# Four stacked blocks on an image batch: the last gated output step and the first convolution half, put under the order of the program

## The chip, the cores and the metric

The kernel runs on one core of a Trainium2 chip. A core has five engines that run their own instruction streams side by side and wait for one another by semaphores: TensorE (PE, matrix products), VectorE (DVE), ScalarE (ACT), GpSimd (POOL) and SyncE (SP, which here only issues DMA transfers). The metric is the time of one execution on the device in microseconds (us), as a median of several runs.

## The reference, cut to what matters

The input `x` is a batch of 8 images of 56 x 56 positions with 192 channels, in float32. Four blocks follow one another, each of the form `x = x + block(group_norm(x))`:

```python
x = x + L0(_gn(x))   # gated Toeplitz mixing, 192 -> 576 -> 192 channels
x = x + L1(_gn(x))   # the same form with other weights
x = x + L2(_gn(x))   # 7x7 depthwise convolution, LayerNorm, 192 -> 768 (gelu) -> 192
x = x + L3(_gn(x))   # shifted window attention, 7x7 windows, 6 heads

def L1(x):           # what the change touches is its last line
    p, q, v = silu(x @ p_w.T + p_b), silu(x @ q_w.T + q_b), silu(x @ v_w.T + v_b)
    o = toeplitz_along_rows(q * v) + toeplitz_along_columns(q * v)
    return (p * o) @ o_w.T + o_b

def L2(x):           # and the first line of this one
    y = depthwise_conv_7x7(x)
    y = gelu(layernorm(y) @ w0 + b0) @ w1 + b1
    return y * gamma
```

## The kernel before, in words

Images go through in pairs: pair `j` is image `j` beside image `j + 4`, so that 192 channels of two images fill three rows of 128 partitions. Two pairs make a half: `j0 = 0` is the first half, `j0 = 2` the second. Each step of work is a Python generator that issues instructions for a while and then yields the time that its author gives to them; `weave` runs one lane of such steps and draws pieces of other work into it after each yield, by those times.

**The order.** All instructions are known when the kernel is built. A planner then sets the order of each engine's stream: it may issue an instruction ahead of others that the program wrote earlier, when its inputs are ready sooner by the planner's own estimates. Inside `tc.manual_schedule(engines=ENGINES)` the four engines PE, ACT, DVE and POOL keep the order in which the program wrote the instructions. SP is not in that set, and its order is the planner's throughout. Before the change such blocks surround the preparation of the tables, the four lanes with the Toeplitz step (`in_order` in `tno_layers`), and the last part of the attention. The fifth lane stands outside of them: `lanes[4]`, the output step `tno_out` of block L1 for the second half (`j0 = 2`), into which `last()` hands the convolution of block L2 for the first half.

**The output step** (`tno_out`) has 28 tiles of 224 positions. For each tile it issues `inner`: 16 matrix products with the gate's weights as 32 instructions (lines 536 and 545) into two PSUM buffers, four silu on ACT (L555), two products by the mixed signal on DVE (L560). Then comes `outer`: the rest of this tile's gate (L575, L581), the normalisation of the next tile's input on DVE (three instructions of L523), the output product of the tile before (L578, L586, L589, L592), one silu (L594) and its product (L595), then bias and residual (L598, L601), the store by POOL's queue (L122) and the statistics for the next group norm (L604). `inner` yields 4.9 and `outer` 5.8, and the convolution is drawn in at these yields. PSUM is cut into four buffers, handed out in turn (`bank2`).

**The convolution** (`conv`) has two kinds of step. A token step (`tokens`, 14 in a half: 7 of part 0 with 128 channels, 7 of part 1 with the other 64) takes a loaded tile `x`, normalises it on ACT (L805: four instructions in part 0, two in part 1), turns it by TensorE transposes (L817: 16 or 8) into PSUM and copies it to `xt` (L828 on DVE, and in part 0 L826 on ACT). There are two buffers of `x`; SP loads the next tile (L791 for part 0, L787 for part 1) when the transposes of the tile two steps back are done. A group step (`group`, 48 in a half) is 16 products by a banded matrix `cm` as 32 instructions (L837) and one ACT copy to `y` (L844). Eight groups fill `y`, of which there is one; POOL copies its border (L878) and stores it to `yd` (L879).

In the text of `tokens` the normalisation stands straight ahead of the transposes that read it:

```python
            for i in range(2 * n):
                j, k = (i, 2) if part else (i // 2, i % 2)
                nc.scalar.activation(x[:, i, :], x[:, i, :], AF.Identity, ...)
            for i in range(0, 4, 2):
                pt = self.bank2()
                ... nc.tensor.transpose(pt[...], x[:, k, ...], self.ident) ...
```

**Where the pieces fall.** Worked out from the yields and from `lo=0.08, hi=0.8` in `last()`, the token steps of part 0 stand after `inner` of tiles 2, 4 and 6 and after `outer` of tiles 2, 3, 4 and 5; those of part 1 after `inner` of tiles 11, 12 and 13, after `outer` of tiles 12 and 13, and two together after `outer` of tile 11. Groups 0 to 15 lie between the two parts, groups 16 to 47 after them, up to `inner` of tile 22. From there on the lane opens the MLP of block L2 (`mlp`, handed in as `after`): the load of `y` (line 920) after `outer` of tile 22, the first half of the LayerNorm statistics (L931, L932: 8 pairs of instructions on DVE) after `inner` of tile 23, the second half and the root (L935 on ACT, L936 on DVE) after its `outer`, and the normalisation (L943, 24 instructions on DVE) after `inner` of tile 24. `last()` also issues the loads of the MLP's vectors and four memsets of `xt` on POOL (L772, L773). After the lane follow the MLP with the second half of the convolution, in the planner's order.

Of the kernel before, what the change touches and what calls it, by code (L numbers as in the profile page):

```python
# [19 lines left out]
ENGINES = {  # L20
    mybir.EngineType.PE,
    mybir.EngineType.Activation,
    mybir.EngineType.DVE,
    mybir.EngineType.Pool,
}
# [13 lines left out]
def view(ap, offset, dims):  # L39

    return bass.AP(ap.tensor, ap.offset + offset, [ap.ap[0], *dims])


class Net:
# [636 lines left out]
    def tno_layers(self, x0, x1, x2, gn, last):  # L681


        tc, nc = self.tc, self.nc
        LS = ("L0", "L1")
        tables = [

            [
                self.dram.tile([D1 // 32 * self.TG + 1, 32 * self.TW], F32, name=f"{L}_tab{d}")
                for d in range(2)  # L690
            ]
            for L in LS
        ]
        qvs = {

            j0: self.dram.tile([D1 // 32, 64 * W, 128], F32, name=f"qv{j0}") for j0 in (0, 2)
        }
        o = [self.dram.tile([B // 2, 9, 128, T], F32, name=f"{L}_sum") for L in LS]
        x = (x0, x1, x2)
        with ExitStack() as ctx, ExitStack() as wqp:  # L700
            self.wqp = wqp.enter_context(tc.tile_pool(name="wqp", bufs=1, side="right"))
            self.tp = ctx.enter_context(tc.tile_pool(name="tp", bufs=3))
            Q = lambda i, j0, *more: self.tno_qv(LS[i], j0, x[i], gn[i], qvs[j0], *more)
            O = lambda i, j0, woven=True: self.tno_out(LS[i], j0, x[i], gn[i], o[i], x[i + 1], gn[i + 1], woven)
            TZ = lambda i, j0: self.tno_toeplitz(j0, tables[i], qvs[j0], o[i])
            QT, OT, TZT = 25 * 2.25 * 5.3, 28 * 10.7, 8 + 72 * 3.2

            with tc.tile_pool(name="tab", bufs=2) as tab:
                stats = [self.input_stats(x0, gn[0], j, tab) for j in range(4)]
                for more in stats[0]:  # L710
                    pass
                first, rest = Q(0, 0, tab, (0, 512)), Q(0, 0, None, (512, 2 * D1), 2)
                next(first)

                for n in range(14):
                    next(first)
                    next(stats[1], None)
                for more in stats[1]:
                    pass
                for n in range(10):  # L720
                    next(first)
                none = tab.tile([112, 512], F32, name="none", bufs=1)
                nc.gpsimd.memset(none, 0.0)
                for t in tables:
                    for d in range(2):
                        nc.gpsimd.dma_start(t[d][D1 // 32 * self.TG :, :512], none[:1])
                decay = [self.decay_tables(LS[i], tab, tables[i]) for i in range(2)]
                more = (dt for st in stats[2:] for dt in st)
                with tc.manual_schedule(engines=ENGINES):
                    for n in range(28):  # L730
                        next(more, None)
                        if n == 18:
                            next(rest)
                        if next(first, None) is None:
                            next(rest)
                        if n < 21:
                            next(decay[0])
                        if n >= 7:
                            next(decay[1])
                        if n in (14, 21):  # L740
                            qv = qvs[0 if n == 14 else 2]
                            to = qv[:, T:].rearrange("n (p k) e -> p n (k e)", p=112)
                            nc.gpsimd.dma_start(to, view(none, 0, [[0, D1 // 32], [1, 512]]))
                    for more in decay:
                        assert next(more, None) is None
                lanes = [[(rest, QT * 5 / 9 * 21 / 25 - 25.0), (Q(0, 2), QT)], [(O(0, 0), OT), (Q(1, 0), QT)]]
                parts = [Q(1, 2, None, cols) for cols in ((0, 512), (512, 2 * D1))]
                lanes += [[(O(0, 2), OT), (parts[0], QT * 4 / 9)], [(parts[1], QT * 5 / 9), (O(1, 0), OT)]]
                lanes += [[(O(1, 2, False), OT)]]
            in_order = tc.manual_schedule(engines=ENGINES)  # L750
            with tc.tile_pool(name="tz", bufs=1) as self.tz, in_order:
                self.tms = []
                for i in range(2):
                    self.tms.append(self.tz.tile([128, 32 * self.TW], F32, name=f"tm{i}"))
                for n, tz in enumerate((TZ(0, 0), TZ(0, 2), TZ(1, 0), TZ(1, 2))):
                    self.weave(lanes[n], tz, lanes[n + 1][0][0], TZT)
                wqp.close()
            self.weave(lanes[4], **last())

# [918 lines left out]
```

## Time and profile before

| what | value |
|---|---|
| median of 3 runs | 5438.96 us (5432.41 to 5443.45) |
| the profiled execution's own time | 5425.63 us |
| its span, first to last instruction | 5423.8 us |
| TensorE busy | 5166.0 us (95%) |
| VectorE, ScalarE, GpSimd busy | 48%, 44%, 33% |
| mean granted TensorE clock | 0.978 |
| fifth lane, from its first to its last matrix product | 3023.97 to 3540.4 us |

The page of a profile gives the busy time of each engine, then the span in 40 equal slices with one digit for each (9 is 90% or more busy), then the chain of work that ended last, then groups of instructions by source line. In a group, "out<-in" names the tiles, and behind the second bar stands how long the engine sat idle just before these instructions and what released it. Views of a stretch of time list the instructions in order: start, duration (of all `xN` together where several stand in one row), engine, line, operation, and in brackets the idle time before. PEld is the load of a weight into TensorE, which overlaps with products. Start and duration are in us from the span's start. Rows of one duration are pipelined, so the next instruction can start before the row's end.

### The profile page before, as it was taken

Reading aid. Unit: us, or ns where it says so; the run is one execution under the profiler, and the core shown is the slowest. Engines: PE = TensorE matmul, PEld = TensorE weight load, DVE = VectorE, ACT = ScalarE, POOL = GpSimd, SP = SyncE. Lnnn points to the kernel's source line nnn. Section 1 sums busy time; section 2 is a strip of 40 time slices with the busy share of each in tenths; the row PEclk is TensorE's granted clock in tenths of the full one; section 3 lists DMA queues with packets and bytes.
Section 4 is the critical chain, followed back from the end, with each engine's and each line's share of the span. In section 5 each row is a group of like instructions: output and inputs, shape, how many; then the busy total and the mean of one; then the engine's idle time right before and its main releaser. Section 6 shows DMA issues by size and latency. Waiting matters only on the chain.

```text
span 5423.8 us, 144350 instructions
## 1 busy us (share of the span) xinstructions
PE 5166.0 (95%) x64672; PEld 3811.2 (70%) x64672; DVE 2589.3 (48%) x3990; ACT 2383.5 (44%) x3179; POOL 1767.2 (33%) x1291
## 2 busy tenths in 40 slices
PE   7879999999999999999999899989999999999998
PEld 4657777777777777777777789856665444777776
DVE  6535556455555555555556422422222331566666
ACT  3345555444554454655455422243323333444443
POOL 2225675133664243546443100000000100333333
PEclk9889999999999999999999999999999999999998
DMA  7699997888786999889897667635454221445552
GB/s 251 151 243 283 289 311 234 265 281 267 241 262 176 307 317 318 279 226 291 285 312 266 205 223 248 229 96 190 135 174 124 75 68 49 85 98 108 101 102 68
DMA packets 1051146, 1116.48 MB, mean 206 GB/s; under 512 B 235200, under 2 KB 986304, under 8 KB 1036128
## 3 DMA queue, kind: packets, MB, share of 16 engines
q1 hardware_dynamic: 911584, 854.88, 52.9%
q0 software_dynamic: 38144, 200.99, 9.6%
q10 hardware_dynamic: 100800, 51.38, 3.9%
q8 instruction: 508, 8.32, 0.6%
q14 instruction: 110, 0.90, 0.1%
HBM read 743.17 MB, written 363.94 MB: 204 GB/s over the span
## 4 chain that ended last, share of the span: by engine, by line
PE 50%; DVE 3%; DMA 3%; issue 1%; ACT 1%; POOL 1%; SPq 0%; POOLq 0%; ACTq 0%; DVEq 0%
PE bank L980 7%; PE bank L837 5%; PE bank L1060 5%; PE bank L1254 4%; PE bank L263 4%; PE bank L592 3%; PE bank L1074 3%; PE bank L536 3%; PE bank L1370 2%; PE bank L1201 2%; PE bank L1284 2%; PE bank L1325 2%; PE bank L406 2%; PE bank L586 1%; PE bank L1344 1%
## 5 line engine op out<-in xcount | busy, mean ns | idle before, releaser
L263 PE MATMUL bank<-wq,t 128*128 128x256 f32 (+4 forms) x7680 | 1290.3, 374 | 72.1 <-DVE t L272 40.8
L263 PEld LDWEIGHTS bank<-wq,t 128*128 128x128 f32 (+2 forms) x7680 | 1005.2, 190 | 350.8 <-issue 92.4
L272 DVE TENSOR_TENSOR t<-bank,wq 128x1024 f32<-128x1024 f32 (+3 forms) x480 | 517.7, 1112 | 692.5 <-PE bank L263 537.1
L304 POOL TENSOR_TENSOR t<-t 128x1024 f32<-128x1024 f32 (+2 forms) x288 | 528.0, 1847 | 676.5 <-ACT t L301 339.1
L413 ACT COPY ot<-bank 128x896 f32<-128x896 f32 x576 | 493.4, 909 | 515.1 <-PE bank L406 401.8
L429 POOL TENSOR_TENSOR s<-s,ot 128x1568 f32<-128x1568 f32 x128 | 551.1, 4306 | 193.8 <-DVE ot L426 128.4
L301 ACT ACTIVATE t<-t 128x2048 f32<-128x2048 f32 (+2 forms) x288 | 423.0, 1488 | 328.8 <-DVE t L272 319.0
L406 PE MATMUL bank<-q,tm 56*32 56x224 f32 x18432 | 504.9, 353 | 22.0 <-DMA tm<-L_tab 10.6
L406 PEld LDWEIGHTS bank<-q,tm 56*32 56x32 f32 x18432 | 340.0, 106 | 148.2 <-issue 81.7
L122 POOL DMA_DIRECT2D x<-t x112 | 87.0, 777 | 1071.7 <-DVE t L601 1007.4
L560 DVE TENSOR_TENSOR t<-t,bank 128x896 f32<-128x896 f32 x224 | 242.8, 1088 | 401.6 <-ACT bank L555 346.0
L555 ACT ACTIVATE bank<-bank,wo 128x448 f32<-128x448 f32 x448 | 262.8, 605 | 377.4 <-PE bank L545 349.8
L980 PE MATMUL bank<-z,w 128*128 128x448 f32 (+1 forms) x1344 | 413.3, 555 | 2.8 <-DVE xt L828 2.8
L536 PE MATMUL bank<-t,wo 128*128 128x224 f32 x1792 | 375.9, 364 | 21.1 <-ACT t L515 10.6
L536 PEld LDWEIGHTS bank<-t,wo 128*128 128x128 f32 x1792 | 337.7, 194 | 51.7 <-issue 29.6
L592 PE MATMUL bank<-t,wo 128*128 128x224 f32 x1792 | 368.9, 359 | 0.0
L592 PEld LDWEIGHTS bank<-t,wo 128*128 128x128 f32 x1792 | 329.9, 190 | 31.1 <-issue 31.1
L980 PEld LDWEIGHTS bank<-z,w 128*128 128x128 f32 (+1 forms) x1344 | 183.0, 189 | 209.8 <-issue 199.5
L837 PEld LDWEIGHTS bank<-xt,cm 113*112 113x112 f32 x3072 | 309.7, 178 | 25.7 <-issue 23.3
L837 PE MATMUL bank<-xt,cm 113*112 113x108 f32 (+2 forms) x3072 | 316.0, 263 | 1.0 <-ACT h L989 1.0
L127 POOL DMA_DIRECT2D x<-x x64 | 36.7, 573 | 855.5 <-DVE x L1011 796.7
L424 DVE STREAM_TRANSPOSE s<-ot 128x1792 f32<-128x1792 f32 x144 | 292.8, 2034 | 24.5 <-ACT ot L413 16.2
(162 smaller groups left out, 6977.2 us busy)
## 6 DMA issues: line engine op xcount, KB each, us to landing
q<-qv SPq DMA_DIRECT2D x36, 3584.0 KB
t<-L_sum SPq DMA_DIRECT2D x112, 1008.0 KB
L_sum<-s POOLq DMA_DIRECT2D x256, 392.0 KB, 7.2
qv<-t SPq DMA_DIRECT2D x192, 512.0 KB
cm<-in_L_cm SPq DMA_DIRECT2D x96, 896.0 KB
tm<-L_tab SPq DMA_DIRECT2D x288, 240.0 KB
q<-qv SPq DMA_DIRECT2D x40, 1568.0 KB
q<-qv ACTq DMA_DIRECT2D x32, 1568.0 KB
```

The lines of the kernel that those rows point to most:

```text
L263: nc.tensor.matmul(pp[:m, b, 256 * j : 256 * j + k], x[rows, j, 2 if part else b, s : s + m], w[rows, part, c0 + c : c0 + c + k],  start=p ...
L272: nc.vector.tensor_add(z[:m, c : c + k, :], view(pp[:m], 0, [[1, k], [256, 4]]), view(bias[:m], c0 + c, [[1, k], [0, 4]]),)
L301: nc.scalar.activation(z[:m, :n, :], z[:m, :n, :], AF.Silu)
L304: nc.gpsimd.tensor_mul(prod[:m, :k], half[:, :, 0], half[:, :, 1])
L406: nc.tensor.matmul(pt[32 * j : 32 * j + 32, r, hf * 224 : (hf + 1) * 224], tm[rows, at : at + 32], q[rows, :, 4 * c : 4 * c + 4], start=Tr ...
L413: nc.scalar.copy(view(ot, 4 * (g % 4), [[16, 2], [32, 112], [1, 4]]), view(pt, 0, [[512, 2], [4, 112], [1, 4]]),)
L424: nc.vector.transpose(to, of.rearrange("p (i k) -> p i k", k=32))
L429: add.tensor_add(to, to, view(of, 0, [[1, 28], [32, 56]]))
L536: mm(gs[c // 2][:, b, c % 2 * 256 : c % 2 * 256 + N], pw[:, 0, 128 * c : 128 * c + 128], xn[:, b], start=c % 2 == 0, stop=False,)
L592: mm(P[:, b, :N], ow[:, c, 0:128], g[:, 4 * b + c], start=False, stop=c == 3)
L837: nc.tensor.matmul(pc[:, 128 * e + 4 * m0 : 128 * e + 4 * m1], cm[:113, e, k, :], xt[:, m0 - 1 + k : m1 - 1 + k, c + e, :], start=n == 0 a ...
L980: nc.tensor.matmul(phs[c][:, s, :TT], w0[rows, part, at : at + 128], z[rows, Z[2 if part else s], :], start=part == flip, stop=part != flip,)
```

## The change

The call of `weave` for the fifth lane is put into a block of its own in which PE, ACT, DVE and POOL keep the order of the program:

```diff
                 for n, tz in enumerate((TZ(0, 0), TZ(0, 2), TZ(1, 0), TZ(1, 2))):
                     self.weave(lanes[n], tz, lanes[n + 1][0][0], TZT)
                 wqp.close()
-            self.weave(lanes[4], **last())
+            with tc.manual_schedule(engines=ENGINES):
+                self.weave(lanes[4], **last())
```

`last()` is evaluated inside the block too, so its memsets belong to it. No instruction is added, removed or altered in its operands.

## The prediction

> **What bounds the kernel now.** I read the page first: the busy slices, and the chain that ended last.
>
> ```profile
> PE   7879999999999999999999899989999999999998
> ...
> PE 50%; DVE 3%; DMA 3%; issue 1%; ACT 1%; POOL 1%; SPq 0%; POOLq 0%; ACTq 0%; DVEq 0%
> ```
>
> TensorE is at nine tenths almost everywhere, and no other engine takes over 3% of the chain. So in the fifth lane (3023.97 to 3540.4) a wait of TensorE is paid in full, and nothing behind the lane has room to give it back: from 3551 to 4101 TensorE is busy 541.62 of 550 us. Then the windows of the lane:
>
> ```profile
> 3023.00:3122.00 99.00, 92.09 (x652) 77.29 (x653) 43.51 (x91) 48.89 (x81) 3.82 (x5) 0.95 0.53 176
> 3122.00:3225.00 103.00, 100.83 (x866) 92.56 (x866) 24.40 (x53) 20.05 (x37) 5.55 (x9) 1.00 0.67 240
> 3225.00:3272.00 47.00, 42.21 (x298) 34.83 (x296) 24.14 (x47) 14.93 (x25) 2.31 (x3) 0.96 0.59 206
> 3272.00:3473.00 201.00, 201.00 (x1746) 183.66 (x1743) 46.83 (x99) 47.22 (x83) 9.60 (x16) 1.00 0.72 252
> 3473.00:3541.00 68.00, 64.25 (x450) 52.17 (x448) 44.87 (x149) 19.94 (x32) 4.60 (x6) 1.00 0.49 153
> ```
>
> Columns are the stretch, its length, then PE, PEld, DVE, ACT, POOL, the granted clock and DMA. TensorE idles 6.9 and 4.8 us in the first and third stretch (the token steps of part 0 and part 1), 2.2 us in the second, nothing in the fourth (groups alone), 3.75 us in the last. The most that a better order can win is these 17.6 us and what a low clock costs after them.
>
> I compared TensorE's order of lines over the whole lane with the order in which the program writes the steps. They agree step for step: the transposes L817 and the products L837 stand where the yields put them. What the planner moved is on ACT and DVE. ACT in order of time:
>
> ```profile
> 3043.87 2.71 ACT L805 ACTIVATE x<-x,gn 128x448 f32<-128x448 f32 x4
> ...
> 3051.23 2.41 ACT L555 ACTIVATE bank<-bank,wo 128x448 f32<-128x448 f32 x4 [3.57 <-PE bank L545]
> ...
> 3081.54 0.76 ACT L805 ACTIVATE x<-x,gn 128x448 f32<-128x448 f32 x1 [3.92 <-DMA x<-x]
> ```
>
> By the program, L805 of the first token step comes behind the silu of 3051.23; here its last two instructions are among those of 3043.87, one to half a tile early. Over the lane L817 waits for L805 nowhere. The price of the early place is the third row: L805 stands ahead of a silu that is ready, and waits there for its transfer. TensorE pays:
>
> ```profile
> 3077.80 1.78 PE L545 MATMUL bank<-t,wo 64*128 64x224 f32 x16
> 3079.51 1.96 PE L817 MATMUL bank<-ident,x 128*112 128x128 f32 x16
> 3085.14 0.63 PE L575 MATMUL bank<-t,wo 64*64 64x224 f32 x1 [3.66 <-DVE t L560]
> ...
> 3092.82 1.91 PE L817 MATMUL bank<-ident,x 128*112 128x128 f32 x16
> 3094.57 0.73 PE L536 MATMUL bank<-t,wo 128*128 128x224 f32 x3
> ```
>
> **The change part by part.** No instruction is added; all cost is waiting.
>
> *Goes: the planner's own waits at the token steps.* Gaps of 3.66, 2.27, 0.76, 1.23, 0.76, 1.34 and 0.70 us, together 10.72, and slow products after two of them: `outer` from 3085.14 takes 7.68 us instead of 6.29, and the transposes and products from 3236.47 lose 0.18 + 1.78. That is 14.1 us off.
>
> *Comes: transposes behind their own normalisation.* In program order ACT runs L805 behind the silu of the half tile just done, and TensorE cannot pass its transposes.
> After `inner`: the silu end 1.77 us after its last product (3051.23 + 2.41 against 3051.87). Four L805 take 2.71, then the last of them lets 13 of 16 transposes go at 0.109 (1.75 over 16, the rows above): 1.42, with 0.1 for the semaphore. 6.0 us instead of 1.75: 4.25 lost, three times, 12.8.
> After `outer`: the silu L594 ends 0.62 after the last product (3073.13 + 0.42 against 3072.93), then the same 2.71 + 0.1 + 1.42: 4.85, so 3.1 lost, four times, 12.4.
> Part 1 has two L805 (1.40) and 8 transposes (0.87, of which 7 remain, 0.76). After `inner` 4.03 against 0.87: 3.16, three times, 9.5. After `outer` 2.88 against 0.87: 2.0, twice, 4.0; the pair behind tile 11 takes 0.62 + 2.80 + 0.1 + 0.76 = 4.28 against 1.74: 2.5.
> Sum 41.2 us. The low end is L805 alone, 7 x 2.71 + 7 x 1.40 = 28.8. The high end adds a transfer of `x` that is late twice, at 6.4 us each (the longest wait of L805 for it): 54. I take 41.2: the next load starts when the transposes two steps back are done, and landed some 6 us later (issued 3094.81, read 3100.60), while a step lasts at least half a tile, 4.85 or 6.29, plus its own wait.
>
> *The clock behind these waits.* Stretches without matrix products in this lane and what the following products lost: 3.57 us before 3023.97 cost 3.1 (6.28 for 16 instructions that take 3.19 later),
>
> ```profile
> 3023.97 6.28 PE L536 MATMUL bank<-t,wo 128*128 128x224 f32 x16 [3.58 <-DVE t L523]
> ```
>
> 5.6 us before 3085.14 cost 1.4, 4.1 us before 3237.86 cost 2.0, 4.2 us before 3116.51 nothing; 2.2 us nothing. Mean of the four above 3.5: 1.6. In program order 11 of 13 places exceed 3.5 us: 11 x 1.6 = 18. Ends: 0 (all like 3116.51) and 11 x 3.1 = 34.
> The Trainium skill, "TensorE: Matmul & The Clock Gate", section "What's actually happening", says that one idle window of about 3.4 us halves the clock and that as long a busy stretch restores it, and its "Part 4: PE-mode transpose" that transposes do not count as busy. By it each of the 11 would cost 1.7 us, 18.7 in all; the window at 3116.51 does not obey it, and the rows decide.
>
> *DVE at the tail.* Before, DVE prepared tile 24 ahead of its wait for the MLP's `y`:
>
> ```profile
> 3475.93 1.00 DVE L523 TENSOR_SCALAR t<-t,gn 128x224 f32<-128x224 f32 x3
> 3478.61 2.25 DVE L560 TENSOR_TENSOR t<-t,bank 128x896 f32<-128x896 f32 x2 [1.68 <-ACT bank L555]
> 3487.08 0.62 DVE L931 BATCH_NORM_STATS2 ln_st<-y 112x6 f32<-112x192 f32 x2 [6.22 <-DMA y<-yd]
> ```
>
> By the program L523 of tile 24 comes behind the first eight pairs of statistics. Let G be the end of the last group (3466.84). The store of `y` (POOL, 3468.14) and the load (SP, 3476.84) bring `y` at G + 20.2 in either order. Eight pairs take 2.6 (11.5 in 3.79), L523 1.0: tile 24 is ready at G + 24.0, while TensorE has ended `outer` 23 at G + 17.4. It starts `inner` 24 there, 4.85 + 1.6 (clock), `outer` 24 ends at G + 36.75. On DVE L560 ends 2.9 behind `inner` 24, at 33.35, L943 takes 6.3 (its row in this stretch), L523 of tile 25 1.0: `inner` 25 starts at G + 40.7, and `outer` 25 ends at 40.7 + 4.85 + 1.6 + 6.3 = G + 53.45. Before it ended at 3510.49 = G + 43.65. So +9.8, with the old waits (1.61, 1.21) netted. Ends: 3.5 (`y` in time) and 15.
> Behind that wait stand on DVE L595, L598, L601, and so POOL's store; ACT's root L935 (with two table loads) stands ahead of the silu of tile 24, but ends by G + 30.3, before those products do.
>
> *Start.* L523 of tile 1 now follows the second L560 (ends 3035.1), four small norm instructions (0.8) and takes 1.0: `inner` 1 at 3036.9 instead of 3034.38, +2.5. Ends 0 and 2.5.
>
> *What costs nothing.* POOL's memsets L772 and L773 (13.2 us) move behind the last store of the lane before (3021.78) and end near 3036; `xt` is first written after 3053. If that cover were gone, at most 13. POOL's stores L122 and L879 keep their mutual order. ACT's waits for `yd` (30.2 us, L844) exist already with TensorE's one gap of 2.17 at 3184; in program order the same PSUM buffer frees at the same time. The loads of `x`, `cm`, the signal (L508) and the vectors are on SP, which is not bound; they follow the buffers that free them.
>
> *Sum.* 41.2 + 18 - 14.1 + 9.8 + 2.5 = +57.4 us. The profiled execution took 5425.63 (span 5423.8 plus 1.8), so its like would be 5483; against the median of the runs shown, 13 higher, 5438.96 + 57.4 = 5496.
>
> **The rivals.**
> *Faster.* Place: the 14 token steps. TensorE's order stays, and only the planner's waits vanish: -14.1, and 2.8 at the tail, 5422. For it: the gaps of 3.66 and 2.27 are made by early L805. It needs less than 14.1 / 14 = 1.0 us of new wait per step; against it, four L805 alone last 2.71.
> *Nothing changes.* The planner could order ACT and DVE in the block as it does now; TensorE's agreement with the program shows how little it moves. 5439. Against: in the fourth lane, which is bound already, ACT keeps the written order (2711.72 L555, 2715.65 L515, 2720.64 L594).
> *Transfers late in order.* If L805 meets its transfer late in seven steps, ACT holds the silu behind it too: 7 x 6.4 = 45 more, 5541. For it: ten waits of L805 for `x` now, 29.3 us. Against: these are waits of instructions that stand early.
> The stretch behind the lane is planned anew; its idle 8 us bound a gain there, and as much may be lost. It lies within the range.
>
> **How the numbers follow.** Forecast 0.80, faster 0.07, nothing 0.05, transfers late 0.08. Measurements of this kernel tell about 0.2%, 11 us. Low end of the forecast: 28.8 + 0 - 14.1 + 3.5 + 0 = +18, 5457; high end 54 + 34 - 14.1 + 15 + 2.5 = +91, 5530. That range leaves out the times of the three rivals and so holds 8 in 10. Slower 0.88, same 0.05, faster 0.07.
>
> **What would show it.** Right: TensorE's order unchanged; L817 (or its weight load) idle some 40 us behind ACT L805, where it is nothing now; L805 always behind L555 or L594; granted clock below 0.95 from 3050 to 3125; one gap of 6 to 7 us ahead of `inner` 24, put down to L523. Wrong: L805 still ahead of the silu, or idle time of L817 below 14 us, or a gain behind 3551.

## The result and the profile after

The changed kernel takes 5487.6 us (median of 4 runs, 5479.48 to 5491.11); the kernel before, on the same chip, 5437.93 (4 runs, 5432.41 to 5443.45). The ratio is 1.0089, interval 1.0072 to 1.0107: the change costs 0.9%, some 50 us.

Lines below the change stand one higher in the new kernel (L806 is the normalisation that was L805, L818 the transposes that were L817). The page after: TensorE's busy share and granted clock in 40 slices, then the chain that ended last.

```profile
PE   7879999999999999999999799899999999999998
...
PEclk9889999999999999999999899999999999999998
...
PE 37%; issue 3%; DVE 2%; DMA 2%; ACT 1%; POOL 0%; POOLq 0%; DVEq 0%; ACTq 0%; SPq 0%
```

The 23rd slice has fallen from 8 to 7, and its clock from 9 to 8; the 26th is now 8. Slices are 137 us long, so these are the first and the last part of the fifth lane. The rest stands as before, but for the 8 that stood in the 27th. TensorE's share of the chain is smaller than before, and no other engine has grown into a bound of the whole; the time in which an engine waits for nothing that the profile shows ("issue") is 3%. The windows of the lane (length, then PE, PEld, DVE, ACT, POOL, granted clock, DMA share, GB/s):

```profile
3035.00:3162.00 127.00, 106.70 (x654) 85.17 (x655) 44.46 (x89) 48.38 (x79) 3.82 (x5) 0.88 0.41 136
3162.00:3260.00 98.00, 96.36 (x836) 88.36 (x835) 23.52 (x50) 19.50 (x36) 4.69 (x7) 1.00 0.67 234
3260.00:3323.00 63.00, 49.90 (x330) 39.32 (x328) 24.77 (x47) 18.52 (x31) 3.17 (x5) 0.95 0.55 193
3323.00:3517.00 194.00, 194.00 (x1690) 178.15 (x1687) 46.98 (x100) 46.15 (x82) 8.74 (x14) 1.00 0.72 248
3517.00:3606.00 89.00, 73.62 (x496) 59.69 (x495) 47.31 (x152) 20.56 (x33) 5.57 (x9) 0.92 0.46 137
```

TensorE now idles 20.3 us in the first stretch (token steps of part 0), 13.1 in the third (part 1) and 15.4 in the last (the tail), and the clock is down in just these three. The stretch of groups alone is full, at clock 1.00, as before.

What TensorE waits for in this lane (us in total, times, longest):

```profile
PE bank L818 <- ACT x L806: 31.6, 41, 2.5
PE bank L536 <- DVE t L523: 19.5, 4, 9.2
```

The first of these waits did not exist before; the second was 3.6. Between two whole profiles much differs that the change has not made: the lane begins at 3035.3 us here, at 3024.0 before, and at 3034.3 in a kernel of the experiments that takes no longer than before. So I compare distances between fixed instructions of the lane. The lane is taken from the first product of `inner` 0 to the first transposes of the MLP behind it; "part 0" from `inner` 2 to `inner` 7, "part 1" from `inner` 11 to `inner` 14, "tail" from `inner` 23 to the lane's end; "hand-over" is from there to the first MLP product (L980 before, L981 after).

| kernel | lane | part 0 | part 1 | tail | hand-over |
|---|---|---|---|---|---|
| before | 516.3 | 78.9 | 47.1 | 67.1 | 10.8 |
| after | 570.4 | 105.9 | 58.4 | 82.1 | 6.1 |
| difference | +54.1 | +27.0 | +11.3 | +15.0 | -4.7 |

`inner` 0 to `inner` 2 adds 1.4 (23.1 to 24.5); the rest of the lane is equal to 0.6 us. Lane and hand-over together are +49.4, the medians differ by 49.7.

The new wait, on ACT in order of time (start, duration of all `xN`, idle before):

```profile
3064.04 2.41 ACT L555 ACTIVATE bank<-bank,wo 128x448 f32<-128x448 f32 x4 [3.57 <-PE bank L545]
3066.38 2.70 ACT L806 ACTIVATE x<-x,gn 128x448 f32<-128x448 f32 x4
...
3078.57 0.42 ACT L594 ACTIVATE bank<-bank,wo 128x224 f32<-128x224 f32 x1 [5.08 <-PE bank L592]
3078.92 2.71 ACT L806 ACTIVATE x<-x,gn 128x448 f32<-128x448 f32 x4
```

and on TensorE:

```profile
3062.96 1.78 PE L545 MATMUL bank<-t,wo 64*128 64x224 f32 x16
3067.18 0.32 PE L818 MATMUL bank<-ident,x 128*112 128x128 f32 x1 [2.43 <-ACT x L806]
3067.83 0.32 PE L818 MATMUL bank<-ident,x 128*112 128x128 f32 x1 [0.33 <-ACT x L806]
3068.48 0.32 PE L818 MATMUL bank<-ident,x 128*112 128x128 f32 x1 [0.33 <-ACT x L806]
3069.13 3.02 PE L818 MATMUL bank<-ident,x 128*112 128x128 f32 x13 [0.33 <-ACT x L806]
3072.08 0.40 PE L575 MATMUL bank<-t,wo 64*64 64x224 f32 x1
```

L806 stands behind the silu of the half tile just done, at each of the 13 places. The first transpose goes when the first of its four instructions is through, two more one by one, and the other 13 with the last. From the end of L545 to L575 pass 7.3 us, where 1.8 passed before. Of the 5.5 us more, 3.4 are idle (2.43 and three times 0.33); the rest is transposes that go one by one or slowly (3.02 for 13 of them, where 16 took 1.96).

### The profile page after: what moved, and what is told of

It reads as the page before. It is cut to its first block, busy times and chain, and to the rows that moved or that the text cites. A ratio compares the mean times of both kernels' runs of the same rounds, so it can differ in the third digit from the quotient of the medians.

```text
span 5489.1 us, 144393 instructions
## 1 busy us (share of the span) xinstructions
PE 5193.2 (95%) x64672; PEld 3826.1 (70%) x64672; DVE 2589.9 (47%) x3990; ACT 2383.7 (43%) x3179; POOL 1767.3 (32%) x1291
## 5 line engine op out<-in xcount | busy, mean ns | idle before, releaser
L413 ACT COPY ot<-bank 128x896 f32<-128x896 f32 x576 | 493.4, 909 | 522.6 <-PE bank L406 416.3
L406 PE MATMUL bank<-q,tm 56*32 56x224 f32 x18432 | 506.9, 354 | 21.6 <-DMA tm<-L_tab 11.3
L555 ACT ACTIVATE bank<-bank,wo 128x448 f32<-128x448 f32 x448 | 263.0, 606 | 395.5 <-PE bank L545 375.6
L981 PE MATMUL bank<-z,w 128*128 128x448 f32 (+1 forms) x1344 | 412.5, 556 | 6.8 <-DMA w<-in_L_w 4.1
L536 PE MATMUL bank<-t,wo 128*128 128x224 f32 x1792 | 378.9, 365 | 34.5 <-DVE t L523 19.5
L981 PEld LDWEIGHTS bank<-z,w 128*128 128x128 f32 (+1 forms) x1344 | 182.5, 189 | 213.2 <-issue 202.9
L424 DVE STREAM_TRANSPOSE s<-ot 128x1792 f32<-128x1792 f32 x144 | 292.8, 2034 | 20.2 <-ACT ot L413 9.4
```

The lines of the kernel that those rows point to most:

```text
L406: nc.tensor.matmul(pt[32 * j : 32 * j + 32, r, hf * 224 : (hf + 1) * 224], tm[rows, at : at + 32], q[rows, :, 4 * c : 4 * c + 4], start=Tr ...
L413: nc.scalar.copy(view(ot, 4 * (g % 4), [[16, 2], [32, 112], [1, 4]]), view(pt, 0, [[512, 2], [4, 112], [1, 4]]),)
L424: nc.vector.transpose(to, of.rearrange("p (i k) -> p i k", k=32))
L536: mm(gs[c // 2][:, b, c % 2 * 256 : c % 2 * 256 + N], pw[:, 0, 128 * c : 128 * c + 128], xn[:, b], start=c % 2 == 0, stop=False,)
L981: nc.tensor.matmul(phs[c][:, s, :TT], w0[rows, part, at : at + 128], z[rows, Z[2 if part else s], :], start=part == flip, stop=part != flip,)
```

## The experiments

A difference between two kernels is read from the ratio of their medians, and its place from the stretches. The kernel before takes 5426 to 5438 us on the different chips, so times of two rows can't be compared as they are, nor a time with an expectation given in us:

| kernel | time | before, same chip | ratio (95%) | lane | part 0 | part 1 | tail | hand-over |
|---|---|---|---|---|---|---|---|---|
| `pe_only` | 5438.63 | 5434.39 | 1.0007 (0.9997 to 1.0017) | 522.6 | 78.8 | 48.5 | 70.7 | 10.5 |
| `no_act` | 5446.73 | 5434.39 | 1.0025 (1.0014 to 1.0036) | 539.0 | 79.1 | 47.3 | 83.0 | 6.0 |
| `no_dve` | 5475.92 | 5434.39 | 1.0080 (1.0065 to 1.0095) | 555.5 | 105.8 | 58.6 | 69.4 | 10.8 |
| `ahead` | 5434.95 | 5434.39 | 0.9999 (0.9988 to 1.0009) | 524.7 | 70.4 | 46.5 | 84.3 | 6.1 |
| `filled` | 5476.95 | 5425.67 | 1.0087 (1.0068 to 1.0106) | 572.9 | 102.4 | 58.9 | 84.9 | 6.1 |
| `filled2` | 5475.65 | 5436.28 | 1.0063 (1.0047 to 1.0078) | 556.7 | 96.1 | 55.4 | 81.3 | 6.1 |
| `twice` | 5522.72 | 5425.67 | 1.0170 (1.0150 to 1.0189) | 614.5 | 128.1 | 74.1 | 81.0 | 6.1 |
| `twice_free` | 5431.44 | 5425.67 | 1.0006 (0.9993 to 1.0019) | 519.0 | 79.3 | 48.2 | 67.8 | 10.7 |
| `both` | 5421.73 | 5425.67 | 0.9990 (0.9978 to 1.0002) | 511.6 | 70.4 | 46.4 | 72.3 | 10.6 |
| `early` | 5428.56 | 5436.28 | 0.9985 (0.9977 to 0.9994) | 508.1 | 70.4 | 46.5 | 69.4 | 10.4 |

### Which engine's order costs it

Three kernels put the block around the lane for some of the engines only. The theory: ACT's written order makes the loss at the token steps, DVE's makes that of the tail, TensorE's makes none. The rival: TensorE's own order, or the block's edges, which cut the planner off from the work around it.

TensorE alone:

```diff
-            with tc.manual_schedule(engines=ENGINES):
+            with tc.manual_schedule(engines={mybir.EngineType.PE}):
                 self.weave(lanes[4], **last())
```

> The block with TensorE alone bound to the written order; ACT, DVE and POOL are the planner's. Theory (TensorE's order was the program's already, the loss is in the orders of ACT and DVE): as before, 5438, within 5428 to 5448. Rival (the block itself costs, by TensorE's order or by the plan behind the lane): 5470 to 5490.

5438.63 against 5434.39, no difference that can be told: by the interval at most some 9 us. The lane of its trace is 6.3 us longer than before, 3.6 of it in the tail, with the planner's waits in other places. Neither the block nor TensorE's order is the cause of the 50 us.

All but ACT:

```diff
-            with tc.manual_schedule(engines=ENGINES):
+            with tc.manual_schedule(engines={mybir.EngineType.PE, mybir.EngineType.DVE, mybir.EngineType.Pool}):
```

> The block binds TensorE, DVE and POOL; ACT is the planner's. Theory (transposes wait for normalisations that ACT may not take early): the token steps cost what they cost before, some 38 us come back against the changed kernel, the tail on DVE stays: 5450, within 5442 to 5460; transposes wait for L806 under 5 us. Rival (DVE's order holds the token steps): 5475 to 5490.

Parts 0 and 1 are back (79.1 and 47.3), the tail is not (83.0). The waits in its lane:

```profile
ACT x L806 <- DMA x<-x: 28.5, 10, 6.0
PE bank L536 <- DVE t L523: 20.3, 4, 9.4
```

ACT again stands early at L806 and waits for the transfer there. That costs TensorE what it cost in the kernel before, whose parts 0 and 1 took 78.9 and 47.1; for L806 itself it waits once, with a weight load, for 0.2 us. What stays is DVE's.

All but DVE:

```diff
-            with tc.manual_schedule(engines=ENGINES):
+            with tc.manual_schedule(engines={mybir.EngineType.PE, mybir.EngineType.Activation, mybir.EngineType.Pool}):
```

> The block binds TensorE, ACT and POOL; DVE is the planner's. Theory: the tail's two waits for L523 (14 us) go, the token steps stay: 5474, within 5466 to 5482; transposes still wait some 30 us for L806. Rival (the tail's wait is the transfer of y and not DVE's order): 5485 to 5491.

The mirror image: parts 0 and 1 as in the changed kernel (105.8 and 58.6), the tail nearly as before (69.4). Its lane:

```profile
PEld bank L818 <- ACT x L806: 42.0, 41, 2.8
...
PE bank L818 <- ACT x L806: 31.6, 41, 2.5
```

By medians the two engines' shares are 41.5 (ACT's order, kept in `no_dve`) and 12.3 us (DVE's, in `no_act`), together 53.9 against the 49.7. No kernel tells POOL's order apart, which is bound in both; the two shares leave nothing for it. The short hand-over goes with the long tail in both.

### Is it the place of the normalisation, or the written order as such?

All four engines stay in the written order, but the text is changed: the normalisation of the next tile is written behind the transposes of this one.

```diff
-        def tokens(part, t, x):
+        def scaled(part, t, x):
             n = 1 if part else 2
             for i in range(2 * n):
...
+        def tokens(part, t, x):
+            n = 1 if part else 2
             for i in range(0, 4, 2):
...
+                if not ahead:
+                    scaled(*tiles[done], xq[0])
                 tokens(*tiles[done], xq.pop(0))
                 done += 1
+                if ahead and done < len(tiles):
+                    scaled(*tiles[done], xq[0])
                 yield 3.6 if part else 5.4
...
         yield from self.all_norms()
+        ahead = j0 == 0
+        if ahead:
+            scaled(*tiles[0], xq[0])
+            yield 2.0
```

> All four engines in the written order, and the program itself written otherwise: each token step of the first convolution half normalises the next step's tile behind its own transposes, and the first tile is normalised one piece earlier. Theory: of the 52 us that the token steps' waits and their clock cost now, at least 40 go: 5443, within 5433 to 5455. Rival (a normalisation put early meets its transfer and holds the silu, as the planner's did): 14 us of that come back, 5455 to 5465.

5434.95, the time of the kernel before, while DVE's tail is still there (84.3). The token steps are not only cured but better than under the planner: 70.4 and 46.5 against 78.9 and 47.1. A token step behind `outer`, on TensorE:

```profile
3066.19 1.91 PE L819 MATMUL bank<-ident,x 128*112 128x128 f32 x16
3067.94 3.19 PE L536 MATMUL bank<-t,wo 128*128 128x224 f32 x16
```

No wait, and the products after it at full speed. The waits left in its lane:

```profile
PE bank L536 <- DVE t L523: 20.7, 4, 10.1
...
PE bank L819 <- ACT x L804: 1.1, 4, 0.3
```

So it is the one step of distance between the normalisation and its reader that was missing, not the written order. The piece added for the first tile also shifts the steps of part 0: five instead of four of the seven now stand behind `outer`, where the forecast priced a wait 1.15 us lower, which is little beside the 47.4 us that parts 0 and 1 have lost against the changed kernel. The result lies at the low end of what was expected of it, since parts 0 and 1 fell below those of the kernel before.

### Doubling the suspected cost

Behind each normalisation stands one more ACT instruction of its size, which copies `x` in place and changes nothing in it. If the transposes wait for ACT, this must cost in the changed kernel and be free in the kernel before.

```diff
                     scale=gn[:, j0 + j, k, 0:1],
                 )
+                if j0 == 0:
+                    nc.scalar.activation(x[:, i, :], x[:, i, :], AF.Identity)
             for i in range(0, 4, 2):
```

In the changed kernel:

> The changed kernel with each token step's normalisation followed by as many copies in place on ACT (four more in part 0, two in part 1; the output is the same). Theory: ACT's time per step is on TensorE's path, 7 x 2.6 + 7 x 1.3 = 27 us more, and some clock: 5517, within 5510 to 5530. Rival (the wait is for the silu or the transfer): under 10 us more, to 5497.

In the kernel before:

> The kernel before with the same copies, in the planner's order. Theory (the planner puts them under products): 5440, within 5433 to 5450. Rival (ACT's time is on the path there too): 5460 or more.

In the planner's order they cost nothing (1.0006), in the written order much: parts 0 and 1 grow by 22.2 and 15.7 us over the changed kernel. The 5522.72 us lie well within the expected range only because this chip is faster: by the ratios (1.0170 against 1.0089) the copies cost 44 us, where 29 were expected. The first row is TensorE's wait in the lane of `twice` (L814 is the copy, L820 the transposes),

```profile
PE bank L820 <- ACT x L814: 54.1, 40, 3.1
```

the next ones all that TensorE's transposes wait for ACT's work on `x` in the lane of `twice_free` (L813 is the copy):

```profile
PEld bank L819 <- ACT x L813: 1.2, 2, 0.9
...
PE bank L819 <- ACT x L813: 0.6, 1, 0.6
...
PEld bank L819 <- ACT x L805: 0.3, 1, 0.3
```

The wait of TensorE has grown by 22.5, the lane by 44.1. The windows of `twice` from `inner` 2 to `inner` 7 and from `inner` 11 to `inner` 14 have

```profile
3059.38:3187.48 128.10, 93.92 (x545) 74.02 (x545) 38.51 (x75) 56.98 (x96) 4.58 (x6) 0.80 0.35 112
3285.38:3359.50 74.12, 53.66 (x298) 41.13 (x297) 24.85 (x46) 26.16 (x44) 3.17 (x5) 0.80 0.46 155
```

a clock of 0.80 in both, where the changed kernel has 0.89 and 0.94. In these two stretches TensorE idles 54.7 us instead of 31.6 and is busy 147.6 us instead of 132.6 with the same work. So of the 37.9 us that they grow by, some 23 are waits and some 15 slower work. The 6.2 us that are left of the lane's growth lie outside of them and were not followed up.

### The share of the clock

To take the slow clock away and leave the wait, products that nobody reads were put ahead of the transposes, as many as fit into the wait of each step, into the PSUM buffer that the transposes then overwrite.

```diff
                 pt = self.bank2()
+                for e in range((5, 4, 4, 5, 4, 4, 5, 4, 2, 0, 4, 2, 4, 2)[7 * part + t] if i == j0 == 0 else 0):
+                    nc.tensor.matmul(
+                        pt[:, 0, :TT],
+                        self.ident,
+                        self.pmat.rearrange("p a b -> p (a b)")[:, :TT],
+                        start=True,
+                        stop=True,
+                    )
                 for r in range(2):
```

A first kernel, `filled`, had one to seven of them, (7, 5, 5, 7, 5, 5, 7, 5, 3, 1, 5, 3, 5, 3):

> The changed kernel with products that nobody reads (1 to 7 of 128 x 128 by 448 per token step, sized to end with the normalisation) put ahead of the transposes, so that TensorE is busy while it waits. Theory (of the 52 us that the token steps' waits cost, about 41 are the waits and the other 11 a halved clock behind them): the waits stay, the granted clock of the token steps is 1, and 11 us go: 5477, within 5470 to 5483. Rival (the clock costs nothing here and all 52 are waits): 5485 to 5495.

The clock went to 1.00 in the token steps, but the lane did not get shorter (572.9). The time is the expected one only because this chip is faster; the ratio, 1.0087, is that of the changed kernel. The cause is the number of products: one such product is two instructions of 0.376 us, seven take 5.3 us, and they outlasted the wait by about 1 us a step. That says nothing on the size of the clock's share. With fewer of them:

> As the filled kernel, with fewer products (2 to 5 per step, none in one) so that they end before the normalisation does. Theory (the waits stay, a halved clock behind them goes): from the start of inner 2 to that of inner 7 97 us, within 95 to 100, where the changed kernel takes 105.9; from inner 11 to inner 14 56 to 57 where it takes 58.4; granted clock 1 in both. Rival (the clock costs nothing in these steps): 104 to 106 and 58 to 59.

The windows of the token steps in `filled2`,

```profile
3057.00:3154.00 97.00, 96.57 (x613) 73.86 (x612) 38.51 (x75) 40.90 (x68) 4.59 (x6) 1.00 0.46 148
3248.00:3304.00 56.00, 55.10 (x339) 40.74 (x338) 23.75 (x46) 18.11 (x30) 3.17 (x5) 1.00 0.56 194
```

and the same steps in the changed kernel:

```profile
3059.00:3166.00 107.00, 88.47 (x552) 70.76 (x551) 38.51 (x75) 40.94 (x69) 4.59 (x6) 0.89 0.42 135
3260.00:3319.00 59.00, 45.90 (x302) 35.66 (x301) 24.14 (x47) 18.09 (x30) 3.17 (x5) 0.94 0.53 184
```

TensorE is busy throughout, does more, at clock 1.00, and is done sooner: part 0 by 9.8 us (96.1 against 105.9), part 1 by 2.9. (Part 1 takes 55.4, a little less than expected.) So 12.7 us of the loss were the clock behind the waits. A product that outlasts the wait makes this figure too small, so it is a low bound; the weight loads of L826 still wait 7.0 us behind L806, so that the overshoot can't be in every step.

The changed kernel's own trace shows the share too. In its parts 0 and 1 the granted clock is either 0.50 or 1.00, and all its changes lie on one grid of 3.4 us. At the first token step of part 0 (a stretch of 7.3 us without products, transposes not counted) it is 0.50 for one such piece, at the fifth (4.6 us) it stays at 1.00:

```profile
3068.70:3072.10 3.40, 3.07 (x17) 2.62 (x16) 0.69 (x1) 0.96 (x2) 0.00 (x0) 0.50 0.00 0
3121.90:3130.20 8.30, 6.12 (x39) 5.24 (x40) 3.61 (x8) 4.22 (x7) 0.76 (x1) 1.00 0.85 291
```

Nine such slow pieces lie in the two parts, at 8 of the 11 stretches that last over 3.5 us. TensorE is busy 29.2 us in them, so half of that, 14.6 us, is what they cost by this count, 1.6 each.

### The tail, and a kernel that is faster than both

`both` is `ahead` with the MLP's first work written later: two more yields between the load of `y` and its statistics, and the normalisation in four pieces.

```diff
         y = load(*tiles[0])
         yield None
+        yield None
+        yield None
...
-        normalize(yn, *y, 0, 4)
-        yield 0.0
+        for m in range(4):
+            normalize(yn, *y, m, m + 1)
+            yield None if m < 3 else 0.0
```

> The kernel with normalisation one token step ahead, all engines in the written order, and in addition the MLP's statistics one tile later and its LayerNorm normalisation in four pieces, one at each yield. Theory (the tail's waits for L523 are DVE standing behind y and behind 24 instructions): the tail shrinks from 90 us to about 70, of which 5 come back at the hand-over to the MLP: 5420, within 5413 to 5427, and faster than the kernel before. Rival (y's transfer holds DVE however late the statistics stand): 5430 to 5437.

The tail falls from 84.3 to 72.3, and the gap ahead of `inner` 24 from 10.1 us in `ahead` (9.22 in the changed kernel) to 0.58. The kernel is as fast as before or a little faster (0.9990, 0.9978 to 1.0002); that it is faster, as expected, is not shown.

`early` moves in addition the normalisation of the next tile (L523) from `outer` to behind `inner`, where nothing is drawn in between:

```diff
             inner(now)
+            if after and not woven:
+                early, after = normalize(*after), None
             yield 4.9
             self.norm_part()
             xn = outer(now, before, after)
+            if not woven and n + 1 < len(tiles):
+                xn = early
```

> The kernel with both changes, and the next tile's normalisation (L523) written behind inner instead of within outer, so that no piece of the MLP stands ahead of it on DVE. Theory (the tail's gap of 3.45 ahead of one inner is DVE's order alone, the start's 1.45 ahead of inner 1 too): no TensorE gap of the lane behind L523 but the first, lane 505 to 508 us where the kernel with both took 511.6; against the kernel before 9 us less in the lane and 0.9970 to 0.9990 in all. Rival (other waits on DVE take its place): lane 510 or more.

5428.56 against 5436.28: 0.9985, 0.9977 to 0.9994. This kernel beats both the changed kernel and the one before, the latter by 8 us (0.15%), with all four engines in the written order. Its lane has of the two waits

```profile
PE bank L536 <- DVE t L523: 7.1, 3, 3.6
...
PE bank L823 <- ACT x L808: 1.1, 4, 0.3
```

where the changed kernel has 19.5 and 31.6. Two waits for L523 besides the first are left, of 0.80 us ahead of `inner` 1 and 2.74 us in the tail, where none was expected, and the lane, 508.1, lies at the upper end of what was.

## Why the prediction was right, point by point

Forecast 5496, measured 5487.6; a loss of 57.4 expected, 49.7 found. The mechanism was that of the forecast; three terms (the clock, the tail, the start) were mis-sized, and one was missing. That the sum comes so near is in part luck: the clock and the start were priced some 6 us too high and the hand-over's 4.7 left out, while the tail was 5.2 too low.

- **TensorE's order unchanged.** Right: `pe_only` takes the time of before.
- **The planner's own waits go (-14.1).** Right. `ahead` takes 9.1 us less for parts 0 and 1 than the kernel before (8.5 and 0.6), and TensorE still idles 4.3 us there. So the planner's waits and what followed them come to some 13.4.
- **Transposes behind their normalisation (41.2) and the clock (18).** With the 14.1 netted, the steps were to add 45.1; they added 38.3 (27.0 and 11.3). So the new cost is 38.3 + 14.1 = 52.4, of which by `filled2` the clock has 12.7 and the waits the other 39.7, against 41.2 from durations of rows and the order of the text alone (the weight loads of L818 idle 41.9 us behind L806 in the lane, where some 40 were to be seen). The clock was mis-sized: it cost 12.7 to 14.6. The 11 stretches over 3.5 us were counted rightly, and 1.6 is what a slow piece costs, but not each of them got one: 8 had one or two, and 3 (of 3.95, 4.05 and 4.61 us) had none. The Trainium skill, "TensorE: Matmul & The Clock Gate", section "What's actually happening", would make it 18.7 by the prediction's estimate if each of the 11 held a whole idle window; but the section calls that window free-running, so a stretch shorter than two windows need not hold a whole one, and the 4.2 us ahead of 3116.51, which the prediction held against the rule, do not contradict it. The one grid of the changes in this trace agrees with that. That such waits bring the clock down is what the windows show (0.89, and 1.00 where the waits are filled).
- **DVE at the tail (+9.8).** Right in kind, too small: +15.0. With G the end of the last group (3517.36 here), the working had `y` at G + 20.2, and it came at G + 22.6; the load was issued 1.0 later after G than before and took 1.3 longer. The eight pairs of statistics took 3.7 instead of 2.6. Then `inner` 24 lost 2.9 us to the clock instead of 1.6, and from its end to `inner` 25 passed 11.7 us instead of 10.2. DVE and TensorE there:

```profile
3539.93 0.36 DVE L932 BATCH_NORM_STATS2 ln_st<-y 112x6 f32<-112x192 f32 x1 [8.55 <-DMA y<-yd]
3540.33 0.18 DVE L933 BATCH_NORM_AGGREGATE mv<-ln_st 112x2 f32<-112x6 f32 x1
3540.43 0.33 DVE L932 BATCH_NORM_STATS2 ln_st<-y 112x6 f32<-112x192 f32 x1
...
3543.65 0.98 DVE L523 TENSOR_SCALAR t<-t,gn 128x224 f32<-128x224 f32 x3
```

```profile
3544.16 6.12 PE L536 MATMUL bank<-t,wo 128*128 128x224 f32 x16 [9.22 <-DVE t L523]
```

  L523 stands behind the eight pairs of statistics, as said, and the gap ahead of `inner` 24 is put down to it; it is 9.22 us, where 6 to 7 were to be seen.
- **Start (+2.5).** 1.4.
- **The hand-over, costed at nothing.** It gave 4.7 back. Before, TensorE waits 9.1 us there for the ACT instruction behind the transposes, which waits for a transfer of `x`; after, it waits 4.1 for a transfer of weights. The short hand-over goes with the long tail (6.0 to 6.1 in the changed kernel, `no_act`, `ahead`, `filled`, `filled2` and `twice`, 10.4 to 10.8 in the others), and not with DVE's written order as such, which `both` and `early` have too. Why the transfers stand otherwise was not tried, and stays open.
- **POOL's memsets.** They were to move behind the last store of the lane before. They did not: that store is at 3033.12 here, and three of the four memsets start ahead of it, the first L773 at 3011.40. The new block did not hold them back behind it. The term was nothing either way.
- **The rivals.** "Faster" fell with the result; it needed new waits below 14 us, and they are 39.7. "Nothing changes" fell with the order on ACT: L806 always behind L555 or L594. "Transfers late" fell too: in the lane of the changed kernel no wait of L806 is put down to a transfer.

The sum with the measured terms: 39.7 + 12.7 - 14.1 + 15.0 + 1.4 - 4.7 = 50.0, against 49.7 of the medians. Its first three terms are by construction the 38.3 us that parts 0 and 1 have grown by; how they divide rests on `filled2` for the 12.7 and on the forecast's rows and `ahead` for the 14.1.

## What to carry to other kernels

Fixing an engine's order at the order of the text makes the distance between a producer and its reader in the text a wait on the chip: before doing it, look in the text for producers that stand straight ahead of their readers on another engine, and price each as producer plus the work queued ahead of it on its engine. Such a wait is cured by writing the producer one step earlier, and then the written order can be the better one, since it doesn't pull instructions so early that they block an engine on a transfer. Price the hand-over at the end of the region too, since the loss of the tail can be given back there in part.

## What was not expected of the hardware

- In the written order, each aggregate (L933) stands straight behind the statistics that it reads, and a pair takes 0.46 us (starts 3539.93 to 3543.65 for eight, the first fence of DVE above). Where the planner put the statistics of the next pair in between, a pair takes 0.32. The instructions last the same, 0.33 and 0.16 to 0.18.
- The clock behind a stretch without products has no fixed price in these runs: nothing behind one of 4.2 us before, 3.1 us behind one of 3.57, and in the changed kernel nothing behind 3 of the 11 and 1.6 us on average for each slow piece of 3.4 us at the other 8. Products whose result nobody reads keep it at 1.00, and in `filled2` the steps with them are faster than those without.
